# Four PSUM banks instead of two for the decays of the first image's scan

## The chip, the cores and the metric

The kernel runs on one core of a Trainium2 chip. The core has five engines that work side by side, each through its own queue of instructions in a fixed order: TensorE (PE; its weight loads are listed as PEld), VectorE (DVE), ScalarE (ACT), GpSimd (POOL) and SyncE (SP), which here issues the DMA transfers. They signal each other with semaphores. PSUM is the small memory that TensorE writes its results to; it has eight banks, and one bank holds 128 x 512 fp32 numbers. GpSimd does not touch it in this kernel. The metric is the device time of one launch in microseconds (us), lower is better.

## The reference

The input is `x` of shape (4, 384, 48, 48), four images of 384 channels and 2304 positions. Four layers follow each other, and each adds to the stream:

```python
x = x + mamba(group_norm(x))                  # layer 0
x = x + fft_filter_conv_gate(group_norm(x))   # layer 1
x = x + depthwise_11x11(group_norm(x))        # layer 2
x = x + mixture_of_experts(group_norm(x))     # layer 3
```

The change is in layer 0. Its core is a recurrence over the 2304 positions, for 768 inner channels with 16 states each:

```python
dA  = exp(dt_t[..., None] * A)                       # the decay
dBx = dt_t[..., None] * B_t[:, None, :] * x_t[..., None]
h   = dA * h + dBx                                   # the scan
y_t = einsum('bds,bs->bd', h, C_t)
```

Ahead of it stand an input projection, a causal convolution over four positions, SiLU, and the projections that give `dt`, `B` and `C`; behind it a gate with SiLU, an output projection and a layer norm. Everything is fp32.

## The kernel before

The images go through layer 0 one after the other. While image b > 0 is in layer 0 (`scans`), the layers 1 to 3 of the images before it (`later` and `experts`) are interleaved in small pieces. While image 0 is in layer 0 there is nothing to interleave: in the loop at the end of `tile_layers`, the queue of such pieces stays empty until image 1 has reached its 24th unit.

An image is cut into five chunks in time of 460 or 464 positions. The 768 inner channels are six groups of 128 partitions, `m`, taken in three pairs, `p`; there are 16 states, `s`. One **unit** (`unit(i, m, s)`, from L614) is one group of channels and one state over one chunk; a chunk has 96, an image 480. In each pair the order is s = 0: m even, m odd; s = 1: m even, m odd; and so on. A unit does this:

- for even m, SP loads the rows B and C of the state, broadcast over the partitions, into `bc` (L622, four buffers);
- ACT writes the decay `da` = exp(a * dt) into a PSUM bank (L626);
- POOL multiplies `bu` = u * B in SBUF (L630, three buffers);
- DVE runs the scan (L634) over `da` and `bu`. For two units of three the result goes back into the bank of `da`. For the third, where `(2 * s + m % 2) % 3` is 0, it goes to `g` in SBUF (six buffers), and the bank is free after the scan;
- where the scan stayed in the bank, DVE multiplies it by C into `g` (L640) and ACT copies the last column to `carry` for the next chunk (L642); the bank is free after both. Where it went to `g`, ACT copies the carry from there (L650), and POOL multiplies by C in place (L651);
- TensorE adds `g` to the sum over the states in PSUM with an identity matrix (L600).

Below, **scan** is L634, **decay** is L626, and **multiply** is L640.

The banks of PSUM in this stage: the pool `mm` has two with the tag `da` for the decays, two with the tag `mm` for all other products of layer 0, and two for the sums (`y0`, `y1`). The pool `bg` has the other two, with the tags `A` and `B`; only `later` and `experts` use them.

Between the units, pieces of other work of layer 0 are put in at set units of the chunk (`plan`): the output projection, the layer norm and the residual of the chunk before (L669 to L714) and the input projection and convolution of the next chunk (L490 to L507), the projection of the gate (L518, L525), at unit 28 `gates` (ACT's SiLU over the convolution of the next chunk, L535, and over this chunk's gate, L538, with a load of an activation table before and behind), at unit 32 `gate` for the first pair (DVE, L659), `expand` and `steps` (L550 to L588, which make `dt` and `u`), and the loads and statistics of the next image (L427, L429).

The order in which the instructions of one engine stand is fixed when the program is built. A list scheduler in the framework takes the instructions in the order of the program as priorities, together with when their operands and buffers would come free by its own estimates, and places the semaphore waits. So a change of the buffers also changes the order on each engine. An engine works its list strictly in this order: an instruction that waits holds up all that is behind it.

Of the kernel before, what the change touches and what calls it, by code (L numbers as in the profile page):

```python
# [9 lines left out]
F32 = mybir.dt.float32  # L10
# [6 lines left out]
P = 128  # L17
# [27 lines left out]
def tile_layers(ctx: ExitStack, tc: tile.TileContext, a: dict, out: bass.AP):  # L45
# [218 lines left out]
    with ExitStack() as first:  # L264
# [61 lines left out]
        with (  # L326
# [4 lines left out]
            for ct in range(CT):  # L331
                t = pp.tile([P, HW], F32, name=f"x0_{ct}")
# [65 lines left out]
        def after(ins, other):  # L398

            tc.add_manual_dep(  # L400
                ins.ins, other.ins.name,
                mybir.DependencyInfo(
                    mybir.DependencyClass.NoSync, mybir.DependencyReason.DATA
                ),
                reason="order",
            )
# [4 lines left out]
                nc.scalar.preload_act_table_set("natural_log_exp_and_others")  # L411
            )

        def scans(wk, mm):


            def bank(name):
# [172 lines left out]
            def summed(i, m, lhsT, src):  # L590

                (b, t), c = G[i], st[i]
                n = CHUNKS[t]
                if ("y", m) not in c:
                    c["y", m] = mm.tile(
                        [P, 512], F32, name=f"y{b}_{t}_{m}", tag=f"y{m % 2}", bufs=1
                    )
                    c["terms", m] = 0
                c["terms", m] += 1
                return nc.tensor.matmul(  # L600
                    c["y", m][:, :n],
                    lhsT=lhsT,
                    rhs=src,
                    start=c["terms", m] == 1,
                    stop=c["terms", m] == DS + 1,
                    skip_group_check=True,
                )
# [7 lines left out]
            def unit(i, m, s):  # L615

                (b, t), c = G[i], st[i]
                n, p = CHUNKS[t], m // 2
                if m % 2 == 0:
                    bc = wk.tile([P, 2, TM], F32, name=f"bc{b}_{t}_{p}_{s}", tag="bc", bufs=4)  # L620
                    c["bct"] = bc
                    nc.sync.dma_start(bc[:, :, :n], c["bc"][:, s, :n].partition_broadcast(P))  # L622
                bc = c["bct"]
                v_ = f"{b}_{t}_{m}_{s}"
                da = mm.tile([P, 512], F32, name=f"da{v_}", tag="da")
                nc.scalar.activation(  # L626
                    da[:, :n], c["dt", p][:, m % 2, :n], AF.Exp, scale=a_neg[:, m, s : s + 1]
                )
                bu = wk.tile([P, TM], F32, name=f"bu{v_}", tag="bu", bufs=3)
                nc.gpsimd.tensor_mul(bu[:, :n], c["u", p][:, m % 2, :n], bc[:, 0, :n])  # L630
                g = wk.tile([P, TM], F32, name=f"g{v_}", tag="g", bufs=6)
                last = carry[:, m, s : s + 1]
                here = da if (2 * s + m % 2) % 3 else g
                nc.vector.tensor_tensor_scan(  # L634
                    here[:, :n], da[:, :n], bu[:, :n], last if t else nil[:, 0:1],
                    ALU.mult, ALU.add,
                )
                late = c.setdefault("late", [])
                if here is da:
                    nc.vector.tensor_mul(g[:, :n], here[:, :n], bc[:, 1, :n])  # L640
                    if t < NC - 1:
                        nc.scalar.copy(last, here[:, n - 1 : n])  # L642
                    ins = summed(i, m, ident, g[:, :n])

                    c["since"] = c.get("since", 0) + 1
                    if late and (c["since"] >= 2 or (m % 2 and s == DS - 1)):
                        after(late.pop(0)(), ins)
                else:
                    if t < NC - 1:
                        nc.scalar.copy(last, here[:, n - 1 : n])  # L650
                    nc.gpsimd.tensor_mul(g[:, :n], here[:, :n], bc[:, 1, :n])  # L651
                    late.append(lambda: summed(i, m, ident, g[:, :n]))
                    c["since"] = 0
# [78 lines left out]
            for i, (b, t) in enumerate(G):  # L732
# [37 lines left out]
                for p in range(MT // 2):  # L770
                    for q in range(2 * DS):
                        unit(i, 2 * p + q % 2, q // 2)
                        for piece in todo.pop(2 * DS * p + q, []):
                            piece()
                        yield b, t, 2 * DS * p + q
# [412 lines left out]
        with (  # L1188
            tc.tile_pool(name="l0", bufs=2) as wk,
            tc.tile_pool(name="l0p", bufs=2, space=PSUM) as mm,  # L1190
            tc.tile_pool(name="lbp", bufs=1, space=PSUM) as bg,
        ):


            queue, share, rate = [], 0.0, 0.0
            for b, t, q in scans(wk, mm):
                last = 2 * DS * (MT // 2) * NC - 1
                at = 2 * DS * (MT // 2) * t + q
                if b and at == 24:
                    assert not queue  # L1200
                    queue = []
                    if b > 1:
                        stack = ExitStack()
                        pool = stack.enter_context(tc.tile_pool(name=f"le{b}", bufs=1))
                        queue += experts(b - 2, pool, bg)
                        queue.append((0, stack.close))
                    queue += later(b - 1, bg)
                    rate = sum(w for w, _ in queue) / (last - at)
                    share = 0.0
                if queue:  # L1210
                    share += rate
                    while queue and share >= queue[0][0]:
                        w, piece = queue.pop(0)
                        share -= w
                        piece()
            for _, piece in queue:
                piece()
# [136 lines left out]
```

## Time and profile before

| what | us |
|---|---|
| median of three runs (5769.63 to 5774.74) | 5773.09 |
| profiled execution, whole time | 5767.51 |
| its span, first to last instruction | 5765.7 |

| engine | busy us | share of the span |
|---|---|---|
| PE | 5255.3 | 91% |
| DVE | 4030.3 | 70% |
| POOL | 3110.3 | 54% |
| ACT | 2956.1 | 51% |

The shares are averages over stages with different limits. The scan of image 0 runs from about 96 us (its first scan instruction) to about 1027 us; after that TensorE fills up with the other layers. In a row of the timeline the columns are the start, the duration, the engine, the line, the operation, what it writes and reads, and how many in a row; in brackets the idle time of the engine before it, and what ended it. In a row of the windows the columns are the window, its length, the busy time of PE, PEld, DVE, ACT and POOL with the number of instructions, TensorE's granted clock, the share of the DMA engines and GB/s.

### The profile page before, as it was taken

How to read it: one execution, taken by the hardware profiler on the slowest of the kernel's cores; microseconds unless marked ns; L12 is line 12 of the kernel's file. 1: busy time of each engine (PE TensorE's matmuls, PEld its weight loads, DVE VectorE, ACT ScalarE, POOL GpSimd, SP SyncE). 2: the span in 40 equal slices, each digit the busy share in tenths (PEclk: the TensorE clock that was granted, in tenths of full speed). 3: DMA queues.
4: the chain of work that ended last, by engine and by line, in shares of the span. 5: the costliest groups of instructions: out<-in, count | busy, mean ns of one | idle time of the engine just before them, and what ended most of it. 6: DMA issues, size and time to landing. Idle time of an engine off the chain costs nothing. (4 is left out here: it accounts for less than half of the span.)

```text
span 5765.7 us, 69035 instructions
## 1 busy us (share of the span) xinstructions
PE 5255.3 (91%) x23236; PEld 3320.9 (58%) x23236; DVE 4030.3 (70%) x5653; ACT 2956.1 (51%) x6424; POOL 3110.3 (54%) x2795
## 2 busy tenths in 40 slices
PE   6888888988889999999887999999988799999999
PEld 3333333433455546777433664877634375789999
DVE  5988988899997796666899577656698856451110
ACT  3555555555566654444655565444455564335321
POOL 3877888766586685555565366545465646000000
PEclk9999989988999999999998899999989899899999
DMA  4444444434344363233333235323332323311100
GB/s 135 134 137 135 143 127 139 124 118 121 118 139 137 114 206 108 89 106 112 112 119 106 90 120 171 99 88 102 103 112 95 121 93 125 114 45 43 54 23 26
DMA packets 396011, 634.19 MB, mean 110 GB/s; under 512 B 32373, under 2 KB 386789, under 8 KB 392190
## 3 DMA queue, kind: packets, MB, share of 16 engines
q1 hardware_dynamic: 382148, 618.58, 33.7%
q10 hardware_dynamic: 13498, 11.11, 0.7%
q8 instruction: 184, 3.01, 0.2%
q14 instruction: 181, 1.48, 0.1%
HBM read 571.80 MB, written 57.80 MB: 109 GB/s over the span
## 5 line engine op out<-in xcount | busy, mean ns | idle before, releaser
L630 POOL TENSOR_TENSOR bu<-u,bc 128x460 f32<-128x460 f32 (+1 forms) x1920 | 2217.2, 1167 | 1346.3 <-DVE g L634 632.8
L600 PE MATMUL y<-g,ident 128*128 128x460 f32 (+1 forms) x3840 | 1838.3, 597 | 286.8 <-DVE g L640 282.2
L626 ACT ACTIVATE da<-dt,a_neg 128x460 f32<-128x460 f32 (+1 forms) x1920 | 1232.1, 646 | 268.5 <-DVE g L640 166.2
L634 DVE TENSOR_TENSOR_SCAN da<-da,carry,bu 128x460 f32<-128x460 f32 (+1 forms) x1008 | 1165.7, 1170 | 196.6 <-ACT da L626 170.1
L600 PEld LDWEIGHTS y<-g,ident 128*128 128x128 f32 x3840 | 704.3, 201 | 1008.1 <-DVE g L640 541.7
L651 POOL TENSOR_TENSOR g<-g,bc 128x460 f32<-128x460 f32 (+1 forms) x660 | 766.7, 1162 | 249.4 <-DVE g L634 128.0
L640 DVE TENSOR_TENSOR g<-da,bc 128x460 f32<-128x460 f32 (+1 forms) x1260 | 775.9, 627 | 109.7 <-PE y L600 80.1
L634 DVE TENSOR_TENSOR_SCAN g<-da,carry,bu 128x460 f32<-128x460 f32 (+1 forms) x528 | 617.2, 1169 | 134.1 <-PE y L600 67.9
L1139 PEld LDWEIGHTS ph<-xe,w 128*128 128x128 f32 x4608 | 596.7, 191 | 54.3 <-issue 40.4
L1157 PEld LDWEIGHTS pout<-hr,w 128*128 128x128 f32 x4608 | 591.4, 190 | 54.7 <-issue 43.8
L1139 PE MATMUL ph<-xe,w 128*128 128x144 f32 x4608 | 620.1, 288 | 0.0
L1157 PE MATMUL pout<-hr,w 128*128 128x144 f32 x4608 | 616.4, 287 | 1.5 <-DVE xe L1168 1.5
L642 ACT COPY carry<-da 128x1 f32<-128x1 f32 x1008 | 158.0, 157 | 884.2 <-DVE g L640 882.5
L998 PEld LDWEIGHTS pc<-band,row 128*128 128x128 f32 x3456 | 455.8, 194 | 81.1 <-issue 48.6
L1147 ACT ACTIVATE hr<-ph,nb 128x144 f32<-128x144 f32 x768 | 235.5, 377 | 507.3 <-PE ph L1139 506.9
L998 PE MATMUL pc<-band,row 128*128 128x162 f32 (+14 forms) x3456 | 469.2, 286 | 6.5 <-ACT row L987 4.7
L669 PE MATMUL po<-w_out,zs 128*115 128x384 f32 (+1 forms) x960 | 346.6, 494 | 11.1 <-DVE zs L659 7.7
L878 DVE SCALAR_TENSOR_TENSOR dw<-pad,w_dw,dw 128x384 f32<-128x384 f32 x576 | 342.2, 609 | 14.4 <-ACT pad L866 11.2
L634 DVE TENSOR_TENSOR_SCAN da<-da,nil,bu 128x460 f32<-128x460 f32 x252 | 291.5, 1170 | 74.3 <-ACT da L626 66.4
L490 PE MATMUL pin<-xch,w_inx 128*128 128x463 f32 (+2 forms) x720 | 323.1, 579 | 10.8 <-DVE dt L585 4.7
L518 PE MATMUL pinz<-xch,w_inz 128*128 128x460 f32 (+1 forms) x720 | 306.0, 559 | 12.0 <-DVE xc L507 7.9
L507 DVE SCALAR_TENSOR_TENSOR xc<-pin,conv_w,xc 128x460 f32<-128x460 f32 (+1 forms) x360 | 246.9, 686 | 76.6 <-ACT xc L502 73.9
(170 smaller groups left out, 4754.8 us busy)
## 6 DMA issues: line engine op xcount, KB each, us to landing
bc<-bcd SPq DMA_DIRECT2D x768, 460.0 KB, 3.6
bc<-bcd SPq DMA_DIRECT2D x192, 464.0 KB, 3.6
xs<-x1d SPq DMA_DIRECT2D x24, 576.0 KB, 4.3
x2d<-xs SPq DMA_DIRECT2D x24, 576.0 KB, 2.9
x<-x2d SPq DMA_DIRECT2D x12, 1152.0 KB, 6.5
x3d<-x SPq DMA_DIRECT2D x12, 1152.0 KB, 5.9
xg<-x3d SPq DMA_DIRECT2D x24, 576.0 KB, 4.6
xe<-x3d SPq DMA_DIRECT2D x64, 216.0 KB, 2.6
```

The lines of the kernel that those rows point to most:

```text
L490: nc.tensor.matmul(ps[:, lo : halo + n], lhsT=w_inx[:, k, bass.ts(j, P)], rhs=c["x"][:, k, lo : halo + n], start=k == 0, stop=k == CT - 1,)
L600: return nc.tensor.matmul(c["y", m][:, :n], lhsT=lhsT, rhs=src, start=c["terms", m] == 1, stop=c["terms", m] == DS + 1, skip_group_check=True,
L626: nc.scalar.activation(da[:, :n], c["dt", p][:, m % 2, :n], AF.Exp, scale=a_neg[:, m, s : s + 1])
L630: nc.gpsimd.tensor_mul(bu[:, :n], c["u", p][:, m % 2, :n], bc[:, 0, :n])
L634: nc.vector.tensor_tensor_scan(here[:, :n], da[:, :n], bu[:, :n], last if t else nil[:, 0:1], ALU.mult, ALU.add,)
L640: nc.vector.tensor_mul(g[:, :n], here[:, :n], bc[:, 1, :n])
L651: nc.gpsimd.tensor_mul(g[:, :n], here[:, :n], bc[:, 1, :n])
L669: nc.tensor.matmul(ps[:w, :C], lhsT=c["zs"][:, m, bass.ts(k, w)], rhs=w_out0[:, m, :], start=m == 0, stop=m == MT - 1,)
L878: nc.vector.scalar_tensor_tensor(v, src, w_dw[:, ct, k : k + 1], v, ALU.mult, ALU.add)
L998: nc.tensor.matmul(d["acc2"][:, : BANDS[k] * W].rearrange("p (h w) -> p h w", w=W)[:, lo - edges[k] : hi - edges[k], xlo:xhi], lhsT=d["row ...
L1139: nc.tensor.matmul(ps[:, bass.ts(m, EB)], lhsT=d["w1"][:, e, k, bass.ts(m, P)], rhs=d["x", s][:, k, :], start=k == 0, stop=k == CT - 1,)
L1157: nc.tensor.matmul(d["o"][:, bass.ts(m, EB)], lhsT=d["w2"][:, e, k, bass.ts(m, P)], rhs=d["h", s, e][:, k, :], start=e == 0 and m == 0 and ...
```

## The change

In image 0 the decays are spread over four banks: by `k = (2 * s + m % 2) % 4`, units with k = 0 or 1 take the two banks of the tag `da` as before, k = 2 takes bank `A`, and k = 3 takes bank `B`. The images 1 to 3 keep the two banks of `da`. Which units scan in place and which scan into `g` is not changed.

```diff
-        def scans(wk, mm):
+        def scans(wk, mm, bg):
...
                 v_ = f"{b}_{t}_{m}_{s}"
-                da = mm.tile([P, 512], F32, name=f"da{v_}", tag="da")
+
+                k = (2 * s + m % 2) % 4
+                if b or k < 2:
+                    da = mm.tile([P, 512], F32, name=f"da{v_}", tag="da")
+                else:
+                    da = bg.tile([P, 512], F32, name=f"da{v_}", tag="AB"[k - 2])
                 nc.scalar.activation(
                     da[:, :n], c["dt", p][:, m % 2, :n], AF.Exp, scale=a_neg[:, m, s : s + 1]
                 )
...
-            for b, t, q in scans(wk, mm):
+            for b, t, q in scans(wk, mm, bg):
```

## Prediction

> **What bounds the kernel now.** I read four views, in this order: the windows (busy time by stretch), the waits of DVE over the scan of image 0, the timeline of a quiet stretch, and the timeline around one `gate`. Then I compared the order of the instructions in the two built programs. That order is the same outside image 0: on PE, ACT, DVE and SP the last four fifths of each list are equal but for buffer numbers, and on POOL the last three quarters. So all that can change lies between the first scan at 96 us and the end of image 0 at about 1027 us.
>
> ```profile
> 352.00:541.00 189.00, 153.68 (x361) 65.68 (x360) 168.04 (x211) 102.98 (x233) 153.70 (x137) 0.95 0.44 137
> ...
> 402.00:421.00 19.00, 14.23 (x33) 6.54 (x32) 18.26 (x22) 11.08 (x27) 18.48 (x18) 0.91 0.45 149
> ...
> 520.00:541.00 21.00, 19.41 (x49) 8.20 (x48) 12.04 (x19) 11.38 (x14) 7.76 (x7) 1.00 0.45 149
> ```
>
> A chunk takes 189 us (first row, from one `gate` to the next). DVE is busy for 168.0 of them and POOL for 153.7; PE (153.7) and ACT (103.0) are further off. The other two rows show that the chunk has parts with different limits. In the middle (402 to 421) POOL is busy for 18.48 of 19.00 us and DVE for 18.26. Ahead of the gate (520 to 541) DVE is busy for 12.04 of 21 us, and POOL for 7.76: there both wait.
>
> ```profile
> DVE zs L659 <- ACT zs L538: 22.7, 5, 4.7
> DVE g L634 <- POOL bu L630: 11.1, 20, 3.0
> DVE da L634 <- ACT da L626: 10.1, 13, 1.5
> DVE xc L507 <- ACT xc L502: 9.2, 8, 3.3
> DVE lnm L689 <- POOL lrs L687: 7.7, 4, 1.9
> ```
>
> These are DVE's longest waits from 96 to 1027 us (total us, times, longest). DVE's whole idle time there is 931.0 - 828.8 = 102 us (the windows); that is the most that any cure of its waits could bring. The decays are named with 10.1 us, but they stand behind others, as the timelines show. First a quiet stretch, DVE and then ACT:
>
> ```profile
> 570.69 1.16 DVE L640 TENSOR_TENSOR g<-da,bc 128x460 f32<-128x460 f32 x2
> 572.27 1.17 DVE L634 TENSOR_TENSOR_SCAN g<-da,carry,bu 128x460 f32<-128x460 f32 x1 [0.42 <-issue]
> 573.36 1.16 DVE L634 TENSOR_TENSOR_SCAN da<-da,carry,bu 128x460 f32<-128x460 f32 x1
> 574.61 0.64 DVE L640 TENSOR_TENSOR g<-da,bc 128x460 f32<-128x460 f32 x1
> ```
> ```profile
> 571.34 0.16 ACT L642 COPY carry<-da 128x1 f32<-128x1 f32 x1 [1.93 <-DVE g L640]
> 571.53 0.65 ACT L626 ACTIVATE da<-dt,a_neg 128x460 f32<-128x460 f32 x1
> ```
>
> DVE waits 0.42 us for a decay that ends at 572.18. That decay stood on ACT behind a carry copy, and the copy behind the first multiply, which freed the bank. So two banks do cost time here, 0.42 us in each period of six units (9.50 us, from 572.27 to 581.77), whatever the profile names as the releaser. Then the gate, DVE, ACT and POOL:
>
> ```profile
> 346.20 1.16 DVE L634 TENSOR_TENSOR_SCAN g<-da,carry,bu 128x460 f32<-128x460 f32 x1
> 352.11 1.18 DVE L659 TENSOR_TENSOR zs<-y,zs 128x460 f32<-128x460 f32 x2 [4.75 <-ACT zs L538]
> 354.28 2.25 DVE L634 TENSOR_TENSOR_SCAN da<-da,carry,bu 128x460 f32<-128x460 f32 x2 [0.99 <-issue]
> ```
> ```profile
> 349.59 2.49 ACT L538 ACTIVATE zs<-zs 128x2760 f32<-128x2760 f32 x1
> 352.10 1.28 ACT L411 ACT_TABLE_LOAD   x1
> ...
> 353.44 0.19 ACT L650 COPY carry<-g 128x1 f32<-128x1 f32 x1
> 353.54 1.22 ACT L626 ACTIVATE da<-dt,a_neg 128x460 f32<-128x460 f32 x2
> ```
> ```profile
> 353.72 1.15 POOL L651 TENSOR_TENSOR g<-g,bc 128x460 f32<-128x460 f32 x1 [5.10 <-ACT carry L650]
> 355.54 2.28 POOL L630 TENSOR_TENSOR bu<-u,bc 128x460 f32<-128x460 f32 x2 [0.67 <-DVE da L634]
> 359.95 1.16 POOL L630 TENSOR_TENSOR bu<-u,bc 128x460 f32<-128x460 f32 x1 [2.13 <-DVE g L634]
> ```
>
> While ACT runs the two SiLUs and the table loads it makes no decays, so DVE runs dry. POOL runs dry too, because its multiply in place waits for a carry copy that is queued behind the SiLUs.
>
> **The change part by part.** No instruction is added or removed. The decays get two more banks, and the order on each engine moves with them.
>
> *Middle of the chunk.* In the new order ACT's decays run two units further ahead of the carries, and DVE does three scans and then two multiplies. The 0.42 us go. POOL is late next: a period has eight POOL operations at 1.12 us from start to start, 8.96 us. From 362 to 440 us POOL is idle for only 78.0 - 76.35 = 1.65 us, so the gain is at most 1.65 us a chunk, 8 us in all. Against it stand the loads of `bc`. A load can start when the last multiply of the pair of units four before is done, and lands 3.3 to 5.9 us after its issue in this stage (58 landings on record, median 3.7). Between the release by POOL's multiply and POOL's next use of the buffer, the old list has at most three POOL operations at 8 places, and the new one at 39. Three operations are 3.36 us, so POOL waits about 0.4 us at each place where it is the limit, some four a chunk: 1.6 us. I take nothing for the middle; ends +8 and -48 (the latter in the rivals).
>
> *The gates, five.* In the new order two more scans and their multiplies stand ahead of the two gate operations (2 x 1.09 + 2 x 0.55 = 3.3 us), with their decays made ahead of the SiLUs. One of them, and three small statistics, now stand ahead of the scan that ACT waits for, so the SiLUs end some 2.6 us later, measured by DVE's work. POOL now has two `bu` products ahead of the multiply that waits for the carry: the products that started at 355.54 (3.4 us after the gate's start) are done before, and the one at 359.95 (7.8 us after) starts when the multiply in place has ended, 2.8 us after. That is 5.0 us earlier, less the 2.6 us, less 0.4 us for a load: 2.0 us each. What follows is limited by POOL (busy for 21.00 of the 21 us from 362 to 383), so POOL's lead counts: 10 us for five. Ends: -13 (only the delay) and +25 (no delay).
>
> *Decays that DVE waits for elsewhere.* 13 waits, 10.1 us, mostly while ACT has other work, and nearly all where DVE is the limit. With two banks in reserve they go; 0.85 us stand at the gate of the last chunk and are counted there. I take 9; ends 0 and 10.
>
> *DVE's own bubbles.* A multiply right behind the scan of the same unit starts 1.25 us after it (573.36 to 574.61); another operation there starts 1.09 us after it (572.27 to 573.36). The old order has 132 such pairs in image 0, the new one 7. Where POOL is the limit that is worth nothing; in the first pair of channel groups of each chunk, where DVE is, it is 48 pairs before and 1 after: 47 x 0.16 = 7.5 us. Ends 0 and 125 x 0.16 = 20.
>
> [...]
>
> *What the new order costs.* Chains of convolution steps of one channel group stand back to back 25 times instead of 18, at 0.72 us a step (2.16 us for three at 66.94) instead of 0.61 with other work between (332.99 to 333.60): 0.8 us. And 120 scans instead of 22 stand at another place than their decay, 49 swaps more: the scan into `g` comes behind a later one, so its carry, POOL's multiply and a `bu` buffer come one scan (1.09 us) later. Where POOL waits for the buffer, the neighbour's comes free 0.13 us after POOL wants one (1.25 - 1.12). Between 0 and 1.09 us each I take 0.08, 4 us, nearest to that; ends 0 and 53.
>
> PE and SP have nothing on the path. PE idles a sixth of the stage, and what queues behind SP's loads of `bc` is counted with them. Layer 1 of image 0 first takes the banks `A` and `B` in image 1, long after the last decay there: nothing, and if that cover were gone a decay's life, some 3 us, once.
>
> Sum: 0 + 10 + 9 + 7.5 - 0.8 - 4 = 21.7, say 22 us. The profiled execution took 5767.5 us with 1.8 us around its span, and would take 5745.5; it lies 5.6 us under the median of the runs, 5773.1, so the forecast for the median is 5751.
>
> **The rivals.** *Hidden anyway:* POOL limits the middle and the gates shift only what waits, so 10 and 7.5 go and 9 shrinks to 5 against 4.8 of costs: 5773. For it speaks POOL's 98% in the middle; against it that POOL idles 35 us a chunk.
>
> *The loads of `bc` become the limit, slower:* at the 39 places a load that lands after 5.9 us instead of 3.7 holds POOL for 5.88 + 0.03 - 3.36 = 2.5 us. At the 19 of them that lie in the POOL-limited part (the second and third pairs), that is 48 us, and 5773 - 22 + 48 = 5799. It decides from 1.2 us a place (22/19). Against it: only five of the 58 landings took over 4.8 us, two over 5.
>
> *More than forecast:* DVE loses most of its waits at the gates, and the bubbles count everywhere: 25 + 10 + 20 - 1 = 54 us, 5719.
>
> *The change does nothing:* ruled out, since the new order does place decays two units further ahead.
>
> **How the numbers follow.** Forecast 0.52, with its own range 5734 to 5764; more 0.10; hidden 0.21; slower by the loads or the swaps 0.17. 0.2% is 11.5 us, about what a measurement of this kernel can tell from no change. The forecast's lower edge falls within that bound with 0.02, so faster is 0.60, same 0.23 and slower 0.17. For 8 in 10 the range runs from 5718, the larger gain, to 5783, into the slower case, leaving out about 0.05 below and 0.12 above.
>
> **What would show it.** Right: the scan of image 0 ends near 1005 us; DVE's 0.42 us waits in the quiet stretch are gone, and POOL has small waits ahead of `bu`; DVE's wait at the gate falls from 4.7 to about 3 us; decays hardly stand among DVE's releasers; POOL's 5.1 us wait ahead of its multiply at the gate shrinks. Wrong: POOL waits for `bc` by the microsecond in the middle, or the chunks still take 189 us from gate to gate. The stages after image 0 should keep their lengths; a difference there would be none that I forecast.

## The result and the profile after

| | median, us | runs |
|---|---|---|
| before | 5767.84 (5757.52 to 5774.79) | 19 |
| after | 5764.0 (5757.6 to 5774.39) | 19 |

The ratio is 0.9995, with a 95% interval from 0.9988 to 1.0002: a change between -7 and +1 us, about -3, where 22 us less were forecast. The profiled execution of after took 5772.02 us, with a span of 5770.2.

Single executions drift by some us in the stages after image 0, whose order is the same in both kernels. So I read image 0 by itself, from 96 us to the start of the first `gate` of image 1 (1108.50 us before, 1107.10 after). That stretch holds the same work in both but for a few instructions at its edges. The windows of before, then of after; columns as in the prediction. After the account, the rows of after are a chunk from `gate` to `gate`, and its two parts.

```profile
96.00:1108.50 1012.50, 848.08 (x2061) 368.27 (x2061) 898.03 (x1135) 549.77 (x1158) 825.38 (x735) 0.94 0.43 134
```
```profile
96.00:1107.10 1011.10, 837.99 (x2059) 368.16 (x2058) 893.71 (x1134) 539.83 (x1155) 822.20 (x734) 0.94 0.42 134
...
352.50:538.40 185.90, 153.12 (x361) 66.06 (x360) 166.45 (x211) 101.20 (x232) 153.20 (x137) 0.94 0.44 140
398.50:417.50 19.00, 13.57 (x30) 5.36 (x28) 17.10 (x23) 8.98 (x23) 17.84 (x17) 0.91 0.47 145
517.40:538.40 21.00, 20.44 (x52) 8.78 (x50) 14.68 (x22) 10.87 (x12) 8.85 (x8) 1.00 0.46 159
```

The stretch is 1.4 us shorter, and even that is not the banks'. The first scan started at 96.03 us before and at 94.28 after, but in the four later runs with two banks (e4, e6, f2, f4) it started at 94.4 to 94.9 us too. So this start varies by itself, and 1.8 us of every lead of after named below were there when the scan began. DVE is busy for 893.7 us instead of 898.0 (4.3 less), and idle for 117.4 instead of 114.5 (2.9 more). The idle time has two parts in the traces: gaps under 0.15 us between neighbours, which the views do not list, fell from 13.5 to 3.7 us, and the longer ones, the waits, rose from 100.9 to 113.7. So DVE's own work, short gaps included, takes 14.2 us less, and the waits took 12.8 of it back. Four banks did not remove waits from DVE; they changed what it waits for. The chunk shown takes 185.9 us instead of 189. In the middle both engines now have more gaps than before (DVE 17.10 of 19 us, POOL 17.84), and ahead of the gate DVE is busy for 14.68 us of 21 instead of 12.04. The waits of DVE from 96 to 1027 us, after:

```profile
DVE da L639 <- POOL bu L635: 41.8, 44, 2.6
DVE zs L664 <- ACT zs L538: 11.5, 5, 2.9
DVE xc L507 <- ACT xc L502: 9.6, 7, 3.6
DVE lnm L694 <- POOL lrs L692: 7.4, 4, 2.0
DVE da L639 <- ACT da L631: 7.3, 9, 1.0
```

The waits for the SiLUs at the five gates fell from 22.7 to 11.5 us, and those that the view puts down to issue (some of the 0.42 us among them) from 11.1 to 1.1. Of these 10 us, some 3 only changed their name: the waits of 1.0 to 1.1 us right behind the gate operations stood under issue before and stand under the decays now. The waits for POOL's `bu` rose from 14.3 us in 25 places to 42.0 in 45 (both kinds of scan). What the first two gave, 18 us, the third took with 28. The same view of POOL, first before, then after:

```profile
POOL bu L630 <- DVE g L634: 63.7, 62, 6.5
POOL bu L630 <- DVE da L634: 41.9, 31, 5.9
POOL g L651 <- ACT carry L650: 17.7, 6, 5.1
```
```profile
POOL bu L635 <- DVE g L639: 49.1, 33, 4.2
POOL bu L635 <- DVE da L639: 34.5, 35, 4.1
POOL g L656 <- DVE g L639: 22.7, 17, 5.8
POOL bu L635 <- DMA bc<-bcd: 16.7, 19, 1.9
POOL g L656 <- ACT carry L647: 13.1, 4, 4.3
```

Before, no load stood among POOL's releasers; after, 19 waits for loads of `bc` do, 16.7 us. And POOL's multiply in place (`g`, L656) waits for DVE twice as long as before, when the row of that kind had 10.9 us. The timeline of DVE after, where the quiet stretch was before:

```profile
564.12 1.18 DVE L639 TENSOR_TENSOR_SCAN da<-da,carry,bu 128x460 f32<-128x460 f32 x1 [0.59 <-POOL bu L635]
565.21 0.62 DVE L645 TENSOR_TENSOR g<-da,bc 128x460 f32<-128x460 f32 x1
565.75 1.16 DVE L639 TENSOR_TENSOR_SCAN g<-da,carry,bu 128x460 f32<-128x460 f32 x1
566.82 0.61 DVE L645 TENSOR_TENSOR g<-da,bc 128x460 f32<-128x460 f32 x1
567.47 1.18 DVE L639 TENSOR_TENSOR_SCAN da<-da,carry,bu 128x460 f32<-128x460 f32 x1
569.69 1.18 DVE L639 TENSOR_TENSOR_SCAN da<-da,carry,bu 128x460 f32<-128x460 f32 x1 [1.04 <-POOL bu L635]
```

The 0.42 us waits are gone, and waits for POOL stand in their place. At the gate shown in the prediction, DVE and then POOL, and below them POOL's wait at the first gate, before and after:

```profile
348.52 1.16 DVE L645 TENSOR_TENSOR g<-da,bc 128x460 f32<-128x460 f32 x2
352.52 1.18 DVE L664 TENSOR_TENSOR zs<-y,zs 128x460 f32<-128x460 f32 x2 [2.85 <-ACT zs L538]
354.83 1.18 DVE L639 TENSOR_TENSOR_SCAN g<-da,carry,bu 128x460 f32<-128x460 f32 x1 [1.12 <-ACT da L631]
```
```profile
345.03 1.17 POOL L635 TENSOR_TENSOR bu<-u,bc 128x460 f32<-128x460 f32 x1 [5.20 <-PE y L600]
...
354.13 1.16 POOL L656 TENSOR_TENSOR g<-g,bc 128x460 f32<-128x460 f32 x1 [4.28 <-ACT carry L647]
356.08 1.16 POOL L635 TENSOR_TENSOR bu<-u,bc 128x460 f32<-128x460 f32 x1 [0.79 <-DVE g L639]
```
```profile
166.00 1.16 POOL L651 TENSOR_TENSOR g<-g,bc 128x460 f32<-128x460 f32 x1 [4.57 <-ACT carry L650]
```
```profile
167.02 1.16 POOL L656 TENSOR_TENSOR g<-g,bc 128x460 f32<-128x460 f32 x1 [1.68 <-ACT carry L647]
```

DVE's wait fell from 4.75 to 2.85 us. POOL's wait for the carry fell only from 5.10 to 4.28 here, and the other long wait, 9 us ahead of it, is as it was (5.20 here, 5.34 before). But this gate is one of the two where POOL gains least. POOL's long wait at the five gates was 4.57, 5.10, 5.11, 4.89 and 5.86 us before (in the last chunk it stands ahead of a product), and is 1.68, 4.28, 4.28, 2.85 and 3.44 after: 25.5 us in all became 16.5.

By the starts of the gate operations in the two timelines (the first one of the last pair of groups), after is ahead by 2.1, 4.2, 6.6, 10.9 and 5.4 us at the ends of the five chunks of image 0, and by 1.4 at the first gate of image 1. So there are three questions: what holds POOL's products back, why the last chunk loses 5.5 us of the lead, and whether the banks are worth anything at all.

### The profile page after: what moved, and what is told of

The parts are those of the page before. It is cut to its first block, busy times and chain, and to the rows that moved or that the text cites. A ratio compares the mean times of both kernels' runs of the same rounds, so it can differ in the third digit from the quotient of the medians.

```text
span 5770.2 us, 68945 instructions
## 1 busy us (share of the span) xinstructions
PE 5252.8 (91%) x23236; PEld 3324.4 (58%) x23236; DVE 4027.8 (70%) x5653; ACT 2948.2 (51%) x6424; POOL 3108.8 (54%) x2795
## 5 line engine op out<-in xcount | busy, mean ns | idle before, releaser
L656 POOL TENSOR_TENSOR g<-g,bc 128x460 f32<-128x460 f32 (+1 forms) x660 | 767.6, 1163 | 256.0 <-DVE g L639 142.5
L674 PE MATMUL po<-w_out,zs 128*115 128x384 f32 (+1 forms) x960 | 346.7, 496 | 12.7 <-DVE xc L507 6.4
L883 DVE SCALAR_TENSOR_TENSOR dw<-pad,w_dw,dw 128x384 f32<-128x384 f32 x576 | 344.5, 613 | 14.4 <-ACT pad L871 11.2
L490 PE MATMUL pin<-xch,w_inx 128*128 128x463 f32 (+2 forms) x720 | 318.9, 574 | 18.3 <-DVE xc L507 8.0
L518 PE MATMUL pinz<-xch,w_inz 128*128 128x460 f32 (+1 forms) x720 | 305.3, 558 | 11.7 <-DVE xc L507 9.0
```

Of the source, the lines that this page charges most:

```text
L490: nc.tensor.matmul(ps[:, lo : halo + n], lhsT=w_inx[:, k, bass.ts(j, P)], rhs=c["x"][:, k, lo : halo + n], start=k == 0, stop=k == CT - 1,)
L674: nc.tensor.matmul(ps[:w, :C], lhsT=c["zs"][:, m, bass.ts(k, w)], rhs=w_out0[:, m, :], start=m == 0, stop=m == MT - 1,)
L883: nc.vector.scalar_tensor_tensor(v, src, w_dw[:, ct, k : k + 1], v, ALU.mult, ALU.add)
```

## The experiments

The theory (A): the banks do give DVE room, and the gain went into the next rings of buffers and into POOL, first the loads of `bc`, then the products `bu`. The rival (B): the two banks were never worth 20 us, or the order itself costs what they bring. In the table the last column is the start of the first gate of image 1 in the profiled execution, against 1108.50 us before.

| run | banks | other change in image 0 | ratio to before (95%) | gate, us |
|---|---|---|---|---|
| after | 4 | | 0.9995 (0.9988 to 1.0002) | -1.4 |
| e1_bc6 | 4 | `bc` 6 | 0.9971 (0.9960 to 0.9981) | -17.8 |
| e2_bu6 | 4 | `bu` 6 | 1.0071 (1.0056 to 1.0086) | +36.7 |
| e3_both5 | 4 | `bc` 5, `bu` 5 | 0.9975 (0.9967 to 0.9984) | -11.7 |
| e4_two_banks_bu6 | 2 | `bu` 6 | 1.0062 (1.0048 to 1.0076) | +35.0 |
| e5_four_noG | 4 | L656 left out | 0.9901 (0.9887 to 0.9916) | -53.5 |
| e6_two_noG | 2 | L651 left out | 0.9997 (0.9988 to 1.0005) | -4.6 |
| e7_first_pair | 4 in the first pair | | 1.0022 (1.0012 to 1.0032) | +3.7 |
| e8_other_pairs | 4 in the other pairs | | 1.0008 (0.9999 to 1.0016) | +1.3 |
| f1_four_bc8bu6 | 4 | `bc` 8, `bu` 6 | **0.9935 (0.9922 to 0.9948)** | -33.7 |
| f2_two_bc8bu6 | 2 | `bc` 8, `bu` 6 | 1.0003 (0.9994 to 1.0011) | -1.7 |
| f3_four_bc8 | 4 | `bc` 8 | 0.9980 (0.9970 to 0.9990) | -21.9 |
| f4_two_bc6 | 2 | `bc` 6 | 1.0006 (0.9996 to 1.0015) | 0.0 |

### Are the loads of `bc` the first thing in the way?

Six buffers instead of four, on the changed kernel (e1), and the same on the kernel before (f4):

```diff
-                    bc = wk.tile([P, 2, TM], F32, name=f"bc{b}_{t}_{p}_{s}", tag="bc", bufs=4)
+                    far = b == 0 and s % 3 == 2
+                    bc = wk.tile(
+                        [P, 2, TM], F32, name=f"bc{b}_{t}_{p}_{s}",
+                        tag="bcx" if far else "bc", bufs=2 if far else 4,
+                    )
```

> Four banks, and in image 0 six buffers for the broadcast rows of B and C instead of four. Theory A (the gain went to the next buffers): in the changed kernel POOL waits 16.7 us at 19 places for these loads, nearly all in the second and third pairs of a chunk, where POOL sets the pace; with six buffers those waits go, and the time falls by 10 to 16 us against the changed kernel, to about 0.9975 of the kernel before. Theory B (the work was only moved, DVE sets the pace): POOL waits as long for scans instead, and the time stays within 3 us of the changed kernel, 0.9995 of the kernel before.

> Two banks and six bc buffers in image 0, the control of the run with four banks and six. Theory A: with two banks no load of bc stands among POOL's waits, so more buffers change nothing: 0.999 to 1.001, 5767 to 5779 us. Theory B (the buffers are worth the 0.3% by themselves, with or without the banks): 0.997.

The two rows of e1, the account of image 0 and DVE's longest wait:

```profile
96.00:1090.72 994.72, 828.40 (x2060) 364.41 (x2059) 891.57 (x1134) 540.07 (x1156) 821.97 (x734) 0.95 0.45 136
```
```profile
DVE da L643 <- POOL bu L639: 24.3, 33, 2.2
```

With six buffers no load is left among POOL's releasers, DVE's waits for `bu` fall from 41.8 to 24.3 us and its idle time from 117.4 to 103.1. From 0.9995 to 0.9971 is 14 us. With two banks the same buffers give nothing (1.0006), so they are worth something only behind the four banks. f4 is a clean control: by its trace the order of the instructions on DVE, ACT and POOL is that of before, item for item. In e1 the order moved in some places against after, so its 14 us need not be the loads' alone. Twice as many additional buffers (f3) is the same as six, within the intervals:

> Four banks, eight bc buffers in image 0, bu as before: the larger dose of the run with six (0.9971, where no load of bc was left among POOL's waits). Theory A: six were enough, so the same as with six: 0.996 to 0.998, 5750 to 5762 us. Theory B (more run-ahead of the loads gives more still): 0.993 or less.

### Is the ring of `bu` next?

Three more `bu` buffers alone, with four banks (e2) and with two (e4):

```diff
-                bu = wk.tile([P, TM], F32, name=f"bu{v_}", tag="bu", bufs=3)
+                far = b == 0 and m % 2 == 1
+                bu = wk.tile(
+                    [P, TM], F32, name=f"bu{v_}", tag="bux" if far else "bu", bufs=3
+                )
```

> Four banks, and in image 0 six buffers for the products u*B instead of three. Theory A: POOL waits some 84 us in image 0 for scans that free such a buffer, most of it ahead of the gates, where DVE has much other work; with six it works ahead there and starts the POOL-limited middle of each chunk some 2 to 4 us earlier, 10 to 20 us in all, about 0.9970 of the kernel before. Theory B: what POOL does ahead it waits for later, since DVE needs its busy time in any case; within 3 us of the changed kernel.

> Two banks as before, and in image 0 six buffers for the products u*B. If the banks matter once POOL has room (theory A), this gains less than the same buffers with four banks: 0 to 8 us against the kernel before, since each period of six units still takes 9.5 us by the loop over two banks. Theory B: the banks never mattered, and it gains as much as with four banks, whatever that is.

Both became slower by 0.6 to 0.7%, some 40 us, which neither theory had expected. Two rows of POOL's waits in e2, then two in e4:

```profile
POOL bu L638 <- DMA bc<-bcd: 129.8, 70, 5.3
POOL g L659 <- ACT carry L658: 20.0, 11, 3.5
```
```profile
POOL bu L633 <- DMA bc<-bcd: 127.0, 90, 4.1
POOL g L654 <- ACT carry L653: 27.5, 20, 3.1
```

With room for more products the scheduler puts more of them ahead of the multiplies in place. Those multiplies hold the `bc` buffers, so each load starts later while POOL wants its data earlier. In the traces of e4 the lists of DVE and ACT are those of before, item for item, and only POOL's differs, so the order of one engine costs this by itself. It needs no fourth bank, and it says that the two rings have to grow together. One or two more of each (e3) brought no more than `bc` alone, with 28 waits for loads left (40.9 us):

> Four banks, and in image 0 five buffers each for the rows of B and C and for the products u*B. Theory A: both waits shrink together, 15 to 30 us less than the changed kernel, about 0.996 of the kernel before. Theory B: within 5 us of the changed kernel.

So the last runs gave both rings enough, in a pool that is closed when image 1 begins: `bc` 4 + 4 by odd and even s, `bu` 3 + 3 by odd and even m. f1 has four banks, f2 two.

```diff
+            only = ExitStack()
+            w0 = only.enter_context(tc.tile_pool(name="l0first", bufs=1))
...
+                if b == 1 and t == 0:
+                    only.close()
...
+                    far = b == 0 and s % 2 == 1
+                    bc = (w0 if far else wk).tile(
+                        [P, 2, TM], F32, name=f"bc{b}_{t}_{p}_{s}",
+                        tag="bcx" if far else "bc", bufs=4,
+                    )
...
+                far = b == 0 and m % 2 == 1
+                bu = (w0 if far else wk).tile(
+                    [P, TM], F32, name=f"bu{v_}", tag="bux" if far else "bu", bufs=3
+                )
```

> Four banks, and in image 0 alone eight buffers for bc (four more, used by odd s) and six for bu (three more, used by odd m), all handed back before image 1. Theory A (the gain of the banks went to POOL, first to the loads of bc that it waits for, then to its order and its own load): with both rings deep enough no load of bc stands among POOL's releasers by more than 5 us, and DVE's waits for bu (24 us with six bc buffers alone) shrink; at least the 0.9971 of six bc buffers alone, 0.993 to 0.997, 5728 to 5752 us. Theory B (a deeper bu ring costs by the order that it gives POOL, products ahead of the multiplies in place, and not by the loads alone): 1.000 to 1.008 as in the run with six bu buffers and four of bc, with DVE or TensorE waiting for POOL's multiplies in place.

> The same eight bc and six bu buffers in image 0 with the two banks of before. Theory A: two banks keep the 0.42 us wait in each period, so the deeper rings are worth nothing by themselves once the loads are out of the way: 0.998 to 1.001, 5761 to 5779 us; the loss of the earlier run with two banks and six bu buffers (1.0062) is gone. Theory B: the loss stays, 1.004 to 1.008.

```profile
96.00:1074.82 978.82, 825.35 (x2059) 358.60 (x2058) 882.98 (x1134) 539.24 (x1155) 820.06 (x737) 0.97 0.44 139
```

f1 takes 5728.55 us, 0.9935 of before, and is faster than both kernels. DVE's idle time in the account is 95.8 us, its busy time 883.0. f2 is at 1.0003: the deeper rings are worth nothing to two banks, and the loss of e4 is gone with the loads' waits. f3 is f1 without the `bu` buffers, and stands at 0.9980: the three `bu` buffers that cost 40 us alone are worth 26 us here by the ratios (21 by the medians).

What the ring of `bu` holds back is plain in the last chunk. DVE and then POOL in after, from the middle of the second pair of groups:

```profile
954.69 1.19 DVE L639 TENSOR_TENSOR_SCAN da<-da,carry,bu 128x464 f32<-128x464 f32 x1 [0.77 <-POOL bu L635]
955.78 0.62 DVE L645 TENSOR_TENSOR g<-da,bc 128x464 f32<-128x464 f32 x1
956.32 1.17 DVE L639 TENSOR_TENSOR_SCAN g<-da,carry,bu 128x464 f32<-128x464 f32 x1
957.41 0.62 DVE L645 TENSOR_TENSOR g<-da,bc 128x464 f32<-128x464 f32 x1
957.94 1.18 DVE L639 TENSOR_TENSOR_SCAN da<-da,carry,bu 128x464 f32<-128x464 f32 x1
959.89 1.19 DVE L639 TENSOR_TENSOR_SCAN da<-da,carry,bu 128x464 f32<-128x464 f32 x1 [0.77 <-POOL bu L635]
```
```profile
953.49 2.28 POOL L635 TENSOR_TENSOR bu<-u,bc 128x464 f32<-128x464 f32 x2
955.96 1.17 POOL L635 TENSOR_TENSOR bu<-u,bc 128x464 f32<-128x464 f32 x1 [0.19 <-DVE da L639]
957.58 1.17 POOL L656 TENSOR_TENSOR g<-g,bc 128x464 f32<-128x464 f32 x1 [0.45 <-DVE g L639]
958.70 2.28 POOL L635 TENSOR_TENSOR bu<-u,bc 128x464 f32<-128x464 f32 x2
```

Three units take 5.20 us here (954.69 to 959.89; the periods before and behind it take 5.22), though POOL has only four operations in them, 4.5 us, and DVE some 4.4. The two engines wait for each other in a ring. DVE's scan at 954.69 needs a product, then comes a multiply, then the scan into `g` at 956.32; POOL's multiply in place at 957.58 waits for that scan (0.45 us); and behind it on POOL's list, at 958.70, stands the product for DVE's next scan at 959.89, which waits 0.77 us. The other wait of POOL, 0.19 us, is for the third `bu` buffer. Before, DVE and then POOL in the same part of the chunk, six units of DVE's list and three of POOL's:

```profile
951.90 1.18 DVE L634 TENSOR_TENSOR_SCAN g<-da,carry,bu 128x464 f32<-128x464 f32 x1 [0.23 <-POOL bu L630]
...
961.28 1.18 DVE L634 TENSOR_TENSOR_SCAN g<-da,carry,bu 128x464 f32<-128x464 f32 x1 [0.23 <-issue]
```
```profile
949.32 1.17 POOL L651 TENSOR_TENSOR g<-g,bc 128x464 f32<-128x464 f32 x1
950.43 3.46 POOL L630 TENSOR_TENSOR bu<-u,bc 128x464 f32<-128x464 f32 x3
953.86 1.15 POOL L651 TENSOR_TENSOR g<-g,bc 128x464 f32<-128x464 f32 x1
```

POOL took 4.54 us for three units, without a wait, and DVE 9.38 us for six, 4.69 for three, with one short wait in six. In f1 DVE does three in 4.32 us, without a wait, and without an idle POOL (its multiplies in place stand 4.5 us apart while it works off a lead):

```profile
921.20 1.17 DVE L646 TENSOR_TENSOR_SCAN g<-da,carry,bu 128x464 f32<-128x464 f32 x1
922.28 0.61 DVE L652 TENSOR_TENSOR g<-da,bc 128x464 f32<-128x464 f32 x1
922.82 2.26 DVE L646 TENSOR_TENSOR_SCAN da<-da,carry,bu 128x464 f32<-128x464 f32 x2
924.98 0.62 DVE L652 TENSOR_TENSOR g<-da,bc 128x464 f32<-128x464 f32 x1
925.52 1.17 DVE L646 TENSOR_TENSOR_SCAN g<-da,carry,bu 128x464 f32<-128x464 f32 x1
```

e1 has the ring of after in the last chunk unchanged (again 9.6 us of waits for `bu` in 12 places there), and its last chunk takes 189.4 us, that of f1 180.4, that of before 184.4.

The Trainium skill, Perfetto Trace Analysis, section Identifying Performance Opportunities, says that the same gap repeating on the engine that should be saturated can mean that there is not enough SBUF or PSUM for the next tile. This case agrees twice: the 0.42 us gap went with two more PSUM banks, and the 0.77 us gap with three more `bu` buffers beside four of `bc`. The run with the `bu` buffers alone shows the limit of such a reading: the ring that the gap points to was the right one, and deepening it alone, without the loads' ring, cost 40 us.

### How much do the banks give when POOL has room?

POOL's multiply in place is left out in image 0, with four banks and with two:

```diff
-                    nc.gpsimd.tensor_mul(g[:, :n], here[:, :n], bc[:, 1, :n])
+                    if b:
+                        nc.gpsimd.tensor_mul(g[:, :n], here[:, :n], bc[:, 1, :n])
```

> Four banks; in image 0 POOL's multiply in place by C is left out, so a third of the terms of the sum lack the factor C. This takes a quarter of POOL's work away and leaves DVE's as it is. Theory A (POOL and its buffers hide the banks): DVE becomes the limit, a period of six units takes about 8.7 us, and the time falls by 30 to 60 us against the kernel before. Theory B (DVE's own work hides them): 0 to 15 us.

> Two banks; the same multiply in place left out in image 0. By theory A the loop over two banks keeps a period of six units at 9.3 to 9.5 us in the middle of a chunk, so this gains only 5 to 15 us, and four banks are worth 20 to 45 us once POOL has less to do. By theory B it gains as much as with four banks, within 8 us.

From 96 to 1027 us this takes POOL's busy time from 770.0 to 594.2 us with two banks, and from 771.7 to 632.5 with four, where more units fall into the window. It gives two banks nothing (0.9997; 5 to 15 us had been expected), and with four banks the time is 57 us under before (0.9901) and 54 under after. So POOL's multiply alone did not hold the kernel before, two banks alone did not either, and each hides the other: with the one in place, taking away the other shows little. What is left out is more than POOL's work: the waits of this multiply for DVE and ACT, and its hold on the `bc` buffers, go with it. f1 tells a part of it: with the multiply in place and both rings deep, four banks give 37 us (0.9935).

### Where in the chunk does it come from?

Four banks only for the first pair of groups (`m < 2`), or only for the other two:

```diff
-                if b or k < 2:
+                if b or k < 2 or m >= 2:
```
```diff
-                if b or k < 2:
+                if b or k < 2 or m < 2:
```

> Four banks in the first pair of channel groups of each chunk alone (the part with the other layer 0 work and the gate), two in the second and third. The gain at the gates and from DVE's waits and bubbles ahead of them was put at 10 + 9 + 7.5 - 5 us; if the step that failed is there, this is within 3 us of the kernel before; if the middle ate it, 15 to 22 us less.

> Four banks in the second and third pairs alone, two in the first. The middle was put at nothing: the waits for the decays (0.42 us a period) go, and waits for the loads of B and C come. Within 4 us of the kernel before if that holds; 8 to 15 us more if the loads cost more than the banks bring there.

Neither part gains: e7 is 13 us slower, which neither of its two expectations had, e8 can't be told from before (+5 us; its interval holds no change), and the two together stand at -3. The parts do not add up. The gate stands at the start of the second pair, so in e7 the SiLUs still cost DVE 22.2 us (five waits), and in e8 12.9; but in e8 the waits for decays, 11.8 us in 14 places, and for `bu`, 29.6 in 31, are higher than before (10.3 in 14, and 14.3 in 25). My reading is that a run-ahead that four banks allow must be given back when the next pair has two; no run shows it. Of the 13 us of e7 only 3.7 stand in image 0 of its profiled execution. Where the others are, in stages whose order is the same, I can't say.

## Why the prediction was right and wrong

The median, 5764.0 us, lies in the range, but that is luck: the range was wide enough to hold the rival *Hidden anyway* (no change; 5773), and the time is that rival's and not the forecast's (5751). The forecast started from 5773, the median of three runs that lie high among the 19 of before (5767.84); 22 us less than these would have been 5746. Two of the gains came about as sized or larger, and were lost in places that the sum had at 0 and at -4.

*Middle, 0.* Right that the 0.42 us would go and that POOL is late next. The loads stood at zero there because they were set against a gain of the same size, at four places a chunk and 0.4 us each, 8 us in all. The number of places was right, 19 where 20 were counted (and 19 by the rival *The loads of `bc` become the limit*). The price was not: they took 0.88 us on average (16.7 us), and the run without them is 14 us faster. The rival's 2.5 us was too high, and its deciding 1.2 us was not reached.

*Gates, +10.* The gain came as sized, and did not last. DVE's waits for the SiLUs fell by 11.2 us, and POOL's long wait at the gate by 1.8 us each (25.5 to 16.5 in all), where the term stood for 2.0. POOL's way from its 25th to its 39th product of a chunk, over the gate, took 183.6 us in the five chunks together instead of 195.4. The step that failed is the next one, that POOL's lead counts because POOL limits what follows. From the 39th product to the 65th, about the rest of the second pair, POOL took 229.8 us instead of 212.8, with 21.1 us of waits instead of 5.1: 5.6 for loads, 12.7 for DVE, 2.9 for a carry. DVE's lead shows the same. By the n-th scan of each list it is 4.0 us at the 20th scan of the third chunk, 6.8 at the 37th (behind the gate), 9.9 at the 47th and 7.5 at the 64th, the last of the second pair; in the last chunk it is 7.6, 7.9, 9.6 and 5.0.

*Decays elsewhere, +9.* Mostly wrong. The view has 10.7 us under the decays after (7.3 at nine scans that stay in the bank, 3.4 at three that go to `g`), against 10.3 before, but without those right behind the gates 9.4 us became 6.4. So 3 us went, not 9. I had seen that these waits mostly fall where ACT has other work, and should have concluded that more banks help little there.

*Bubbles, +7.5.* Too small, and hidden. In the trace of before, 130 multiplies stand right behind the scan of the same unit without a wait, and start 1.25 us after it on average; what else stands behind a scan without a wait, 330 operations, starts after 1.08. In after, 5 of the former are left. DVE's own work, short gaps included, took 14.2 us less in after and 26.3 us less in f1, of the 33.7 that f1 gains by its gate. So in f1 the larger part of the gain is DVE's own time and the smaller part, 7.4 us, is waits. No run isolates the term: two banks with the new order on DVE were not tried.

*Swaps, -4 between 0 and 53.* This is the term that was mis-sized most. I priced a carry and a `bu` buffer that come one scan later at 0.08 us each, by one buffer's margin on POOL. The two engines close a ring instead, and lose 0.5 us in every three units where it stands (5.20 against 4.69). With the loads out of the way (e1) DVE still waits 24.3 us for `bu` in 33 places, and the deeper ring of `bu` is worth 26 us behind eight `bc` buffers (f3 to f1, 0.9980 to 0.9935), where the term had 4. The convolution chains' -0.8 was not measured by itself.

*What is handed back.* Not in the prediction: from the end of image 0 to the first gate of image 1 the lead falls from 5.4 to 1.4 us. Two steps of the convolution have moved behind the last gate there, and the banks are two again.

The sum then reads: the rival *More than forecast* (54 us) is about what the banks can give, as the pair without POOL's multiply shows (57 against 2 us); two rings and POOL's multiply in place took nearly all of it. Of the signs that were named, the gone 0.42 us, the small waits of POOL ahead of `bu`, the 3 us at the gate and the unchanged order of the later stages came; the end of the scan at 1005 us (it was near 1020), a DVE that hardly waits for decays, and much less of POOL's wait at the gate shown (it is 4.28 us) did not. One sign of being wrong came in part: POOL waits for `bc`, for up to 1.9 us.

## What to carry to other kernels

When a ring of buffers is deepened, follow the run-ahead to the next ring and the next engine before counting the gain: here PSUM banks, `bc` and `bu` together gave 0.65%, the banks alone nothing that can be measured, and the ring of `bu` alone cost 0.7%. Price a swap in an engine's list by the loop that it closes with the other engine, not by one operation's margin. And where two engines are both busy for nearly all of a stretch (here 18.3 and 18.5 of 19 us), test a cure with the second engine relieved: it tells a cure that does nothing from one that is hidden.

## What had not been expected of the hardware

- Two engines with 4.5 and 4.4 us of work for three units took 5.20 to 5.22 us for them, three periods in a row, through three waits of 0.19 to 0.77 us of which none by itself looks like a limit.
- Three more buffers for `bu`, with the order that came of them, made POOL wait 127 us for DMA loads where two banks had no such wait (e4), and 130 us where four banks had 16.7 (e2).
- The first 1100 us of a profiled execution and the whole times can disagree by some 5 to 10 us, with the same orders behind: a lead of 21.9 us at the first gate of image 1 (f3) stood against 12 us by the ratio and 14 by the medians, and a lag of 3.7 us (e7) against 13 and 9. The first 1100 us seem the finer measure: f4, whose order is that of before, reached that gate at the same time within 0.1 us, while its whole times spread over 26 us. But that is one profiled execution of each, and why the two disagree stays open.
